# Block attention: neighbours laid beside each row from SBUF, rotation on VectorE, the sum over keys in halves

## The chip, the cores and the metric

The kernel runs on one core of a Trainium2 chip. A core has five engines that run their own instruction streams: TensorE (PE, with its weight loads as PEld), VectorE (DVE), ScalarE (ACT), GpSimd (POOL) and SyncE (SP). SP computes nothing here: it issues nearly all DMAs (SPq in the profile), in program order; an issue that waits for a semaphore holds back all those behind it. SBUF is the on-chip memory of 128 partitions, PSUM takes the matmuls' results, DRAM is outside. The metric is device time in microseconds (us) for the whole program; smaller is better.

## The reference, cut to what matters

The program is one layer with three parts: cross attention, block attention and a gated FFN, each added to x. The change lies in the block attention. There are 16 sequences of 64 rows with H = 256, so 1024 rows; 16 heads of 16 dimensions; 8 blocks a sequence, so a block has 8 rows, and each row attends to at most the 8 rows of its own block.

```python
def _L0_attn_ref(x, ...):
    bt = S // NB                                      # 64 / 8 = 8
    h = rmsnorm(x, attn_norm_w)
    qkv = bitlinear(h, qkv_w).reshape(B, S, 3, NH, HD)
    ...
    q = apply_rope(q, cos, sin)
    k = apply_rope(k, cos, sin)
    qb, kb, vb = (blk(q), blk(k), blk(v))             # blocks of bt rows
    scores = jnp.einsum('bnhqd,bnhkd->bnhqk', qb, kb) * scale
    scores = jnp.where(causal, jnp.finfo(scores.dtype).min, scores)
    attn = jax.nn.softmax(scores, axis=-1)
    ctx = jnp.einsum('bnhqk,bnhkd->bnhqd', attn, vb)
    ...
    x1 = x + bitlinear(ctx, o_w)
    hn = rmsnorm(x1, ffn_norm_w)
    gate, val = jnp.split(hn @ ffn_up_w.T, 2, axis=-1)
    return x1 + bitlinear(jax.nn.silu(gate) * val, ffn_down_w)

x = x + _L0_xattn_ref(_layernorm(x), ctx_2048, ...)   # self attention, and 1601 context keys a sequence
x = x + _L0_attn_ref(_layernorm(x), ...)
x = x + _L0_ffn_ref(x, ...)
```

`apply_rope` rotates pairs of dimensions by the row's position: x1 cos - x2 sin and x2 cos + x1 sin. `bitlinear` quantizes its input per row to 8-bit integers (`act_quant` in the kernel) and its weights to -1, 0, 1.

## The kernel before, in words

The 1024 rows are 8 tiles of 128 rows, one row on each partition. Each tile goes through the cross attention part (self attention, then 13 chunks of 128 context keys for each of four units of a tile), the block attention with its small FFN (`last_parts`, L1005), and the gated FFN. The cross attention fills TensorE: for each chunk it projects keys (`ps_k` L624), stores them to DRAM and reads them back transposed (`kd<-kh` L655, `kT<-kd` L665, both issued by SP), forms scores (`s` L696), takes running maxima on VectorE (L715), subtracts the maximum (`mx`, loaded from DRAM in L750; L754), exponentiates on ScalarE (L758) and accumulates (`acc` L772) against context rows loaded by SP (`ctxN` L617; `ctxT` L608 is the transposed copy that the projection reads). A tile's block attention is laid over the cross attention of the tile after it. Only the last tile (7) has none to lie over: there `fill()` calls put matmul chunks of the last FFN between its steps.

The order is made in two layers. All work is emitted by generators on a heap: a generator says by `yield w` how many steps later it goes on, and a list of offsets by the index of the yield (`PACE["last"]`, and `PACE["last_tile"]` for tile 7) shifts each of them. A tile framework then places the instructions on each engine's stream and adds the semaphore waits. Taking one yield out thus moves everything behind it in the same generator by a step, and each later yield takes the offset of its new index.

The block attention of a tile of rows, in order:

- L1023 and L1028: q and k (`qk`, 512 wide) and `v3` (256 wide) come from PSUM to SBUF on ScalarE.
- L1035: GpSimd multiplies `qk` by cos into `r1`; L1041: VectorE multiplies the swapped halves by sin into `r2`, two instructions of 128x256; L1046: VectorE adds them, so that `r1` holds the rotated q (first 256) and k (last 256).
- L1051: two DMAs write k (from `r1`) and v to a DRAM tile `kv`.
- L1060 (`near`): for k and for v, two tiles of 128x1024 each (one for each half of the heads) in which every row holds the 8 rows of its block side by side. A tile takes 8 DMAs: DMA k fills the partitions t = k of all 16 blocks. Each reads 16 lines of 4 KB (a block's 8 rows of 512 B lie in a row in DRAM). So 32 DMAs for each tile of rows, 64 KB each, all from SP; in tile 7 every second one of k's is issued by ScalarE instead.
- L1066 and L1067 (`product`): VectorE multiplies q by the neighbours' k and sums over the 16 dimensions into `sc` (128x128: head, key), twice; softmax L1082 to L1093; then the same function multiplies `sc` by the neighbours' v and sums over the 8 keys into `cx`, twice. The second sum reads its tile in the order head, dimension, key, so with a stride.
- L1096 to L1110: `cx` is quantized (`am`, `asc`, `aq_u`, `aq_q` L980 to L989), transposed on TensorE (`tr_aq` L997) and multiplied by the output weights (`po_o` L1110); then the FFN (`hn`, `ps_g`, `ps_u` L1129, `po_d` L1141) and in the end `out` (L1223).

The tiles `near` and `prod` share the ten buffers of the pool `wp` with the pieces of weights that SP loads.

Of the kernel before, what the change touches and what calls it, by code (L numbers as in the profile page):

```python
# [14 lines left out]
F32 = mybir.dt.float32  # L15
# [4 lines left out]
ALU = mybir.AluOpType  # L20
AX = mybir.AxisListType
PSUM = bass.MemoryType.PSUM

P = 128
B, S, H = 16, 64, 256
# [48 lines left out]
def body(tc, ctx, a):  # L74
    nc = tc.nc
    V, A, PE, GP = nc.vector, nc.scalar, nc.tensor, nc.gpsimd
# [9 lines left out]
    dram = ctx.enter_context(tc.tile_pool(name="dram", bufs=2, space=bass.MemoryType.DRAM))  # L86
# [753 lines left out]
    def fill(where):  # L840
        n = FILL.get(where, 0)
        for fn in late[:n]:
            fn()
        del late[:n]
# [97 lines left out]
    def b1(name, dt=F32):  # L942
        return one.tile([P, 256 if dt == F32 else 512], dt, tag="b1", name=name, bufs=4)

    def b2(name):
        return one.tile([P, 512], F32, tag="b2", name=name, bufs=3)
# [58 lines left out]
    def last_parts(i, start):  # L1005
        need(8, "x", i)
        last = i == NT - 1
# [4 lines left out]
        h = b1("h")  # L1012
# [14 lines left out]
        v3 = b1("v3")  # L1027
# [4 lines left out]
        if last:  # L1032
            fill("rope")
        r1, r2 = b2("r1"), b2("r2")
        GP.tensor_tensor(  # L1035
            r1.rearrange("p (h d) -> p h d", h=32), qk.rearrange("p (h d) -> p h d", h=32),
            rope[:, 0:16].unsqueeze(1).to_broadcast([P, 32, 16]), ALU.mult,
        )
# [7 lines left out]
        V.tensor_tensor(r1, r1, r2, ALU.add)  # L1046
        yield 1

        kv = dram.tile([2, 2, P, P], F32, tag="kv3", name="kv3")
        for e, t in ((0, r1[:, H : 2 * H]), (1, v3)):  # L1050
            nc.sync.dma_start(out=kv[e].rearrange("a p c -> p a c"), in_=t.rearrange("p (a c) -> p a c", a=2))  # L1051
        yield 1

        def near(e, a):
            t = wp.tile([P, 1024], F32, tag="w", name="near")
            src = kv[e, a].rearrange("(n j) c -> n (j c)", j=8)
            for k in range(8):

                q = nc.scalar if last and e == 0 and k % 2 else nc.sync
                q.dma_start(out=t.rearrange("(n t) x -> n t x", t=8)[:, k, :], in_=src)  # L1060
            return t

        def product(out, x, y, order):

            t = wp.tile([P, 1024], F32, tag="w", name="prod")
            V.tensor_tensor(t.rearrange("p (h j d) -> p h j d", h=8, j=8), x, y, ALU.mult)  # L1066
            V.reduce_sum(out, t.rearrange("p (h j d) -> p " + order, h=8, j=8), axis=AX.X)  # L1067

        near_k = [near(0, a) for a in range(2)]
        yield 2  # L1070
        sc = one.tile([P, 16, 8], F32, tag="sc3", name="sc3")
        for a in range(2):
            if last:
                fill("sc%d" % a)
            product(
                sc[:, 8 * a : 8 * a + 8, :],
                r1[:, a * P : (a + 1) * P].rearrange("p (h d) -> p h d", h=8).unsqueeze(2).to_broadcast([P, 8, 8, 16]),
                near_k[a].rearrange("p (j h d) -> p h j d", j=8, h=8), "h j d",
            )
            yield 1  # L1080
        near_v = [near(1, a) for a in range(2)]
        V.tensor_tensor(sc, sc, cmask.unsqueeze(1).to_broadcast([P, 16, 8]), ALU.add)  # L1082
        mx = small.tile([P, 16], F32, tag="mx3", name="mx3", bufs=2)
        V.reduce_max(mx, sc, axis=AX.X)
# [10 lines left out]
        cx = one.tile([P, H], F32, tag="cx3", name="cx3")  # L1095
        for a in range(2):  # L1096
            if last:
                fill("av%d" % a)
            product(
                cx[:, a * P : (a + 1) * P].rearrange("p (h d) -> p h d", h=8),  # L1100
                sc[:, 8 * a : 8 * a + 8, :].unsqueeze(3).to_broadcast([P, 8, 8, 16]),
                near_v[a].rearrange("p (j h d) -> p h j d", j=8, h=8), "h d j",
            )
            yield 1
        to = ternary_piece(1536, 512).rearrange("p (k o) -> p k o", k=2)
# [176 lines left out]
    for i in range(NT):  # L1282
        base = 52 * i
        for hh in range(2):
            for bb in range(2):
                unit(i, hh, bb, base + 26 * hh + 13 * bb)
            spawn(base + 26 * hh + 13 + 34 - 2 + (2, 1)[hh], 6.5, paced("pair", pair_out(i, hh, 4 if i < NT - 1 or hh == 0 else None)))
        ln0, sa0, qx0 = SCHEDULE[i] if i in SCHEDULE else (
            base - 22, [base + o for o in (-15, 0, 8, 21)], [base + o for o in (-16, -7, 15, 18)]
        )  # L1290
        spawn(ln0, 1.0, paced("ln" if i else "ln_first", ln_tile(i)))
        for p in range(4):
            spawn(sa0[p] - 2, 5.0, paced("sa", self_attention(i, p)))
            spawn(qx0[p] - 2, 3.0, paced("qx", queries(i, p)))
        l0 = base + {NT - 3: 95, NT - 2: 88, NT - 1: 82}.get(i, 90)
        spawn(l0, 4.5, paced("last" if i < NT - 1 else "last_tile", last_parts(i, l0)))
    spawn(-8, 1, bias_rows())
    spawn(60, 5.7, ternary())
    order = [(kind, p) for p in range(4) for kind in ("wq", "wkv", "wqx", "wproj")]
# [76 lines left out]
```

## Time and profile before

| quantity | value |
|---|---|
| median of 3 runs | 2389.42 us (2388.86 to 2392.49) |
| the profiled execution | 2387.51 us |
| its span on the core | 2385.7 us |
| instructions | 40447 |
| mean granted TensorE clock | 0.99 |
| share of the 16 DMA engines, main queue | 74.7% (682904 packets, 481.91 MB) |

The span runs from the first to the last instruction of the profiled execution; the time of the execution is 1.8 us longer. TensorE, VectorE, ScalarE, GpSimd and SyncE overlap, so shares of busy time do not add up to a time: what counts is where TensorE is idle and what ends that. The durations of the block attention's own operations, summed over all 8 tiles (the columns are line, engine, operation, tiles and shapes, count, then busy time in us and the mean of one in ns, then the idle time before them):

```profile
L1067 DVE TENSOR_REDUCE cx<-prod 128x128 f32<-128x1024 f32 x16 | 29.7, 1886 | 0.1
L1066 DVE TENSOR_TENSOR prod<-r,near 128x1024 f32<-128x1024 f32 x16 | 19.4, 1218 | 4.9 <-DMA near<-kv 4.9
L1067 DVE TENSOR_REDUCE sc<-prod 128x64 f32<-128x1024 f32 x16 | 19.3, 1211 | 0.0
L1066 DVE TENSOR_TENSOR prod<-sc,near 128x1024 f32<-128x1024 f32 x16 | 19.0, 1218 | 0.9 <-DMA out<-ot 0.8
...
L1041 DVE TENSOR_TENSOR r<-qk,shp 128x256 f32<-128x256 f32 x16 | 13.1, 826 | 6.3 <-ACT qk L1023 6.3
...
L1046 DVE TENSOR_TENSOR r<-r,r 128x512 f32<-128x512 f32 x8 | 5.5, 693 | 0.3
```
```profile
L1035 POOL TENSOR_TENSOR r<-qk,shp 128x512 f32<-128x512 f32 x8 | 10.5, 1311 | 6.8 <-ACT qk L1023 6.7
```

### The profile page before, as it was taken

To read this page: it belongs to the slowest core of one execution; us is meant where nothing else is said; L and a number is where in the kernel's file an instruction comes from. 1 tells how busy PE (TensorE), PEld (TensorE's weight loads), DVE (VectorE), ACT (ScalarE), POOL (GpSimd) and SP (SyncE) were. 2 spreads that over 40 slices of the span, in tenths; PEclk is the share of its full clock that TensorE was granted. 3 is DMA by queue.
4 is the path that set the end of the run, shared out by engine and by line. 5 is a ranking of instruction groups with operands and counts; after the bars stand their busy time and mean duration, and the time that the engine had idled before them with its cause. 6 is when DMAs were issued, how large, how long until landed. Compare 5 with 4: busy or idle time off the path is not lost.

```text
span 2385.7 us, 40447 instructions
## 1 busy us (share of the span) xinstructions
PE 2315.7 (97%) x12469; PEld 1761.8 (74%) x12477; DVE 1849.4 (78%) x4786; ACT 1663.3 (70%) x3712; POOL 755.7 (32%) x968
## 2 busy tenths in 40 slices
PE   7999999999999999999999999999999999999995
PEld 4577777777787777777777777777777777677774
DVE  7677768878878788687887779877887877876766
ACT  4677767776777777767776777777687676777620
POOL 3333223332332333332432423333333433332200
PEclk9999999999999999999999999999999999999997
DMA  8989868777977688776887769776797766965323
GB/s 263 267 236 263 235 175 240 207 186 183 269 206 196 175 229 241 197 207 181 237 224 195 203 174 260 208 196 186 185 267 199 203 174 183 262 169 141 116 85 111
DMA packets 683662, 485.18 MB, mean 203 GB/s; under 512 B 464476, under 2 KB 592952, under 8 KB 683448
## 3 DMA queue, kind: packets, MB, share of 16 engines
q1 hardware_dynamic: 682904, 481.91, 74.7%
q8 instruction: 100, 1.64, 0.3%
q14 instruction: 114, 0.93, 0.1%
q10 hardware_dynamic: 544, 0.69, 0.1%
HBM read 271.03 MB, written 113.11 MB: 161 GB/s over the span
## 4 chain that ended last, share of the span: by engine, by line
PE 79%; DVE 8%; DMA 4%; ACT 3%; issue 3%; POOL 1%; SPq 1%; ACTq 0%; DVEq 0%; POOLq 0%
PE acc L772 25%; PE ps_k L624 24%; PE s L696 14%; PE po_p L332 2%; PE po_x L863 2%; PE ps_q L379 2%; DMA kd<-kh 2%; ACT P L706 1%; PE tr_pc L799 1%; PE tr_q L399 1%; PE ps_kv L379 1%; PE sc L490 1%; DVE P L754 1%; PE pgu L1197 1%; DMA kT<-kd 1%
## 5 line engine op out<-in xcount | busy, mean ns | idle before, releaser
L772 PEld LDWEIGHTS acc<-ctxN,P 128*128 128x128 f32 (+1 forms) x4160 | 713.0, 190 | 212.5 <-issue 132.2
L772 PE MATMUL acc<-ctxN,P 128*128 128x257 f32 (+5 forms) x4160 | 799.2, 338 | 5.1 <-DMA ctxN<-in_ctx_n 2.9
L624 PE MATMUL ps_k<-wkx,ctxT 128*128 128x512 f32 x1600 | 761.1, 598 | 13.9 <-DVE wkx L1269 9.3
L567 POOL TENSOR_SCALAR vx<-ss 128x4 f32<-128x4 f32 x402 | 168.1, 418 | 1196.8 <-DVE ss L564 785.5
L706 ACT ACTIVATE P<-s,rsx 128x128 f32<-128x128 f32 x1536 | 439.6, 373 | 148.2 <-PE s L696 136.0
L568 POOL TENSOR_TENSOR rsx<-vx,nhalf 128x4 f32<-128x4 f32 x402 | 444.1, 1105 | 32.4
L624 PEld LDWEIGHTS ps_k<-wkx,ctxT 128*128 128x128 f32 x1600 | 277.8, 192 | 211.2 <-issue 190.3
L696 PE MATMUL s<-qx,kT 128*128 128x128 f32 x3072 | 411.6, 277 | 4.7 <-ACT qn L389 2.8
L696 PEld LDWEIGHTS s<-qx,kT 128*128 128x128 f32 x3072 | 377.4, 192 | 22.9 <-issue 5.3
L715 DVE TENSOR_TENSOR M<-P,M 128x512 f32<-128x512 f32 (+1 forms) x384 | 263.0, 685 | 163.1 <-ACT P L706 142.0
L651 ACT COPY kh<-ps_k 128x1024 uint16<-128x1024 uint16 x360 | 366.2, 1017 | 7.1 <-DMA kd<-kh 7.0
L758 ACT ACTIVATE P<-P 128x512 f32<-128x512 f32 (+1 forms) x416 | 266.4, 641 | 146.4 <-DVE P L754 144.8
L559 ACT ACTIVATE sq<-ps_k 128x512 f32<-128x512 f32 x402 | 242.6, 603 | 165.6 <-PE ps_k L624 141.5
L564 DVE TENSOR_REDUCE ss<-sq 128x4 f32<-128x512 f32 x402 | 272.1, 677 | 23.4 <-ACT sq L559 23.0
L754 DVE TENSOR_TENSOR P<-P,mx 128x512 f32<-128x512 f32 (+1 forms) x416 | 283.2, 681 | 0.0
L226 POOL TENSOR_TENSOR rs<-ve,nhalf 128x4 f32<-128x4 f32 (+2 forms) x112 | 116.0, 1038 | 254.0 <-DVE ve L223 239.8
L232 DVE TENSOR_SCALAR qn<-qn,mv,rs 128x128 f32<-128x128 f32 x256 | 77.2, 339 | 47.5 <-POOL rs L226 46.9
L219 DVE BATCH_NORM_STATS2 st<-qn 128x6 f32<-128x128 f32 x256 | 64.5, 271 | 21.4 <-ACT qn L389 21.3
L310 DVE TENSOR_TENSOR wproj<-wproj,w_hi 128x1024 fp32r<-128x1024 f32 x60 | 73.0, 1217 | 9.7 <-ACT w_hi L309 9.7
L309 ACT CAST w_hi<-wproj 128x1024 fp32r<-128x1024 f32 x60 | 63.3, 1056 | 24.2 <-DMA wproj<-wproj 20.4
L332 PE MATMUL po_p<-wproj,cat 128*128 128x256 f32 x272 | 67.0, 293 | 0.0
L332 PE MATMUL po_p<-w_hi,cat 128*128 128x256 f32 x240 | 65.7, 308 | 0.8 <-ACT qk L1023 0.8
(239 smaller groups left out, 2751.8 us busy)
## 6 DMA issues: line engine op xcount, KB each, us to landing
kd<-kh SPq DMA_DIRECT2D x375, 256.0 KB
ctxT<-in_ctx SPq DMA_DIRECT2D x192, 256.0 KB
ctxN<-in_ctx_n SPq DMA_DIRECT2D x384, 128.0 KB
wproj<-wproj SPq DMA_DIRECT2D x68, 512.0 KB
wq<-wq SPq DMA_DIRECT2D x32, 512.0 KB
wkv<-wkv SPq DMA_DIRECT2D x32, 512.0 KB
wqx<-wqx SPq DMA_DIRECT2D x32, 512.0 KB
near<-kv SPq DMA_DIRECT2D x248, 64.0 KB
```

Of the source, the lines that this page charges most:

```text
L332: PE.matmul(po[:, 0:H], lhsT=cat[:, h, :], rhs=w[:, h * H : (h + 1) * H], start=h + e == 0, stop=h == 3 and e == len(ws) - 1,)
L559: A.activation(sq[:n], ps[:n], AF.Square)
L564: ordered("dve", V.reduce_sum(ss[:n], sq[:n].rearrange("p (g d) -> p g d", g=4), axis=AX.X))
L568: ordered("pool", GP.tensor_tensor(rs[:n], ve[:n], nhalf[:n, 0:4], ALU.pow))
L624: PE.matmul(ps[:n, :], lhsT=st["cxT"][c // 2][:, k, o : o + n], rhs=wkx[:, k, 512 * hh : 512 * (hh + 1)], start=k == 0, stop=k == 1,)
L651: A.copy(t, src.bitcast(U16).rearrange("p (c e) -> p e c", e=2))
L696: PE.matmul(ps[:n, g * P : (g + 1) * P], lhsT=kT[:, g, 0:n], rhs=qxs[i, hh][:, bb, 2 * g : 2 * g + 2, :].rearrange("p h s -> p (h s)"), st ...
L706: A.activation(pc[:, g * P : (g + 1) * P], ps[:, g * P : (g + 1) * P], AF.Copy, scale=rs[:, g : g + 1])
L715: ordered("dve", V.tensor_tensor(st["M"][:n], pc[:n], st["M"][:n], ALU.max))
L754: ordered("dve", V.tensor_tensor(pc[:n], pc[:n], st["mx"][:n].rearrange("p g q -> p (g q)"), ALU.add))
L758: A.activation(pc[:n], pc[:n], AF.Exp)
L772: m = PE.matmul(ps, lhsT=pc[:n, g * P : (g + 1) * P], rhs=cx[:n, o : o + w], start=g < 3 and c == 0, stop=c == NC - 1, skip_group_check=g ...
```

## The change

Three things are changed in `last_parts`.

1. The product with cos moves from GpSimd (`GP`) to VectorE (`V`).
2. The DRAM tile `kv`, its two writes and the `yield 1` behind them are gone. `near` reads its neighbours from SBUF, from `r1` or `v3`: a DMA takes all 128 partitions of one half of the heads (128 floats, 512 B each) and writes them as 16 lines of 8 pieces. A DMA still moves 64 KB, in 128 pieces of 512 B where it was 16 of 4 KB. The number of DMAs, their engines and the alternation in tile 7 stay. The entries of the lists `PACE["last"]` and `PACE["last_tile"]` are not edited, so the yields behind the removed one take the entries one place earlier.
3. The sum over the 8 keys (`cx`) is made of three additions on the product's own tile: 64 + 64 elements for each of 8 heads (512 in all), then 32 + 32 (256), then 16 + 16 (128) into `cx`. The sum over dimensions (`sc`) stays a reduction.

```diff
--- before.py
+++ after.py
@@ -1032,7 +1032,7 @@
         if last:
             fill("rope")
         r1, r2 = b2("r1"), b2("r2")
-        GP.tensor_tensor(
+        V.tensor_tensor(
             r1.rearrange("p (h d) -> p h d", h=32), qk.rearrange("p (h d) -> p h d", h=32),
             rope[:, 0:16].unsqueeze(1).to_broadcast([P, 32, 16]), ALU.mult,
         )
@@ -1046,39 +1046,37 @@
         V.tensor_tensor(r1, r1, r2, ALU.add)
         yield 1
 
-        kv = dram.tile([2, 2, P, P], F32, tag="kv3", name="kv3")
-        for e, t in ((0, r1[:, H : 2 * H]), (1, v3)):
-            nc.sync.dma_start(out=kv[e].rearrange("a p c -> p a c"), in_=t.rearrange("p (a c) -> p a c", a=2))
-        yield 1
-
-        def near(e, a):
+        def near(src, a, both):
             t = wp.tile([P, 1024], F32, tag="w", name="near")
-            src = kv[e, a].rearrange("(n j) c -> n (j c)", j=8)
             for k in range(8):
 
-                q = nc.scalar if last and e == 0 and k % 2 else nc.sync
-                q.dma_start(out=t.rearrange("(n t) x -> n t x", t=8)[:, k, :], in_=src)
+                q = nc.scalar if both and k % 2 else nc.sync
+                q.dma_start(
+                    out=t.rearrange("(n t) (j c) -> n t j c", t=8, j=8)[:, k], in_=src[:, a * P : (a + 1) * P]
+                )
             return t
 
-        def product(out, x, y, order):
+        def product(x, y):
 
             t = wp.tile([P, 1024], F32, tag="w", name="prod")
             V.tensor_tensor(t.rearrange("p (h j d) -> p h j d", h=8, j=8), x, y, ALU.mult)
-            V.reduce_sum(out, t.rearrange("p (h j d) -> p " + order, h=8, j=8), axis=AX.X)
-
-        near_k = [near(0, a) for a in range(2)]
+            return t
+
+        near_k = [near(r1[:, H : 2 * H], a, last) for a in range(2)]
         yield 2
         sc = one.tile([P, 16, 8], F32, tag="sc3", name="sc3")
         for a in range(2):
             if last:
                 fill("sc%d" % a)
-            product(
-                sc[:, 8 * a : 8 * a + 8, :],
+            t = product(
                 r1[:, a * P : (a + 1) * P].rearrange("p (h d) -> p h d", h=8).unsqueeze(2).to_broadcast([P, 8, 8, 16]),
-                near_k[a].rearrange("p (j h d) -> p h j d", j=8, h=8), "h j d",
+                near_k[a].rearrange("p (j h d) -> p h j d", j=8, h=8),
+            )
+            V.reduce_sum(
+                sc[:, 8 * a : 8 * a + 8, :], t.rearrange("p (h j d) -> p h j d", h=8, j=8), axis=AX.X
             )
             yield 1
-        near_v = [near(1, a) for a in range(2)]
+        near_v = [near(v3, a, False) for a in range(2)]
         V.tensor_tensor(sc, sc, cmask.unsqueeze(1).to_broadcast([P, 16, 8]), ALU.add)
         mx = small.tile([P, 16], F32, tag="mx3", name="mx3", bufs=2)
         V.reduce_max(mx, sc, axis=AX.X)
@@ -1096,10 +1094,14 @@
         for a in range(2):
             if last:
                 fill("av%d" % a)
-            product(
-                cx[:, a * P : (a + 1) * P].rearrange("p (h d) -> p h d", h=8),
+            t = product(
                 sc[:, 8 * a : 8 * a + 8, :].unsqueeze(3).to_broadcast([P, 8, 8, 16]),
-                near_v[a].rearrange("p (j h d) -> p h j d", j=8, h=8), "h d j",
+                near_v[a].rearrange("p (j h d) -> p h j d", j=8, h=8),
+            ).rearrange("p (h x) -> p h x", h=8)
+            for n in (64, 32):
+                V.tensor_tensor(t[:, :, 0:n], t[:, :, 0:n], t[:, :, n : 2 * n], ALU.add)
+            V.tensor_tensor(
+                cx[:, a * P : (a + 1) * P].rearrange("p (h d) -> p h d", h=8), t[:, :, 0:16], t[:, :, 16:32], ALU.add
             )
             yield 1
         to = ternary_piece(1536, 512).rearrange("p (k o) -> p k o", k=2)
```

## The prediction

> **What bounds the kernel now.** I read the busy line first, then a table of stretches, one for each row tile of 128 rows (columns: PE, PEld, DVE, ACT and POOL busy, granted clock, DMA share, GB/s).
>
> ```profile
> PE 2315.7 (97%) x12469; PEld 1761.8 (74%) x12477; DVE 1849.4 (78%) x4786; ACT 1663.3 (70%) x3712; POOL 755.7 (32%) x968
> ```
> ```profile
> 740.00:1025.00 285.00, 282.47 (x1555) 217.33 (x1555) 228.29 (x591) 209.10 (x464) 94.12 (x119) 1.00 0.78 210
> ...
> 2163.00:2280.00 117.00, 112.28 (x637) 90.73 (x637) 79.95 (x152) 74.53 (x174) 26.00 (x34) 0.97 0.44 129
> 2280.00:2386.00 106.00, 79.66 (x395) 63.20 (x394) 63.88 (x160) 15.42 (x32) 3.60 (x5) 0.88 0.28 89
> ```
>
> PE is idle for 70 us of 2385.7: 26 in the last 106, 4.7 in the stretch before, 17 at the start. A middle stretch of 285 loses only 1.5 to 4. The change deletes no matmul, so it can be paid only in idle PE time that block attention causes. Two views find that time. Windows of 10 us:
>
> ```profile
> 870.00:880.00 10.00, 8.62 (x52) 6.68 (x51) 9.36 (x20) 6.87 (x15) 1.37 (x2) 1.00 1.12 264
> ```
>
> The same window in six tiles (from 585, 870, 1155, 1440, 1715, 2020) has PE busy 8.01, 8.62, 9.51, 8.85, 8.68, 8.07: 8.3 us lost in all. SP's timeline and the chain of waits say why:
>
> ```profile
> 853.46 10.54 SPq L1060 DMA_DIRECT2D near<-kv  x16
> ...
> 864.72 1.45 SPq L665 DMA_TRANSPOSE kT<-kd  x1
> ```
> ```profile
> 867.83 6.45 DMA kT<-kd
> ```
>
> Sixteen loads of v's neighbours hold SP for 10.5 us; the transposes of context keys (kT) queued behind them start late, and the scores on PE wait for one (867.83 to 874.28). DVE meanwhile runs the four operations of the v product (L1066, L1067) without a break, 6 us, which holds back the softmax work that PE needs. The second place is tile 6, window 2265 to 2275 (PE 6.28 of 10): PE's waits give 4.0 us at tr_aq L997 for DVE's aq_q L989, the quantizer behind cx. The third is the tail, below.
>
> **The change part by part. The tail (tile 7), where little covers it.** The chain and the timeline of before:
>
> ```profile
> 2328.49 0.36 SPq L1051 DMA_DIRECT2D kv<-r  x1
> ...
> 2330.37 15.30 SPq L1060 DMA_DIRECT2D near<-kv  x24
> ```
> ```profile
> 2345.08 2.24 DMA near<-kv
> ...
> 2348.06 1.24 DVE prod L1066
> 2349.32 1.87 DVE cx L1067
> 2351.21 0.43 DVE am L980
> ```
>
> 24 issues on SP (8 of k, 16 of v) take 15.30, or 0.637 each; ScalarE's queue issues the other 8 of k. The last lands 2.24 us after its issue, then DVE multiplies, sums, quantizes.
> (a) Rotation. Before: POOL's product 1.27 (L1035) beside two halves that took 1.66 instead of 2 x 0.42, then the sum 0.69. After, all on DVE: 0.60 (128x512, start to start) + 0.34 + 0.34 = 1.28, plus one late FFN operation (0.34) that the new order puts between: 1.62. r1 is ready as before: 0.
> (b) The hop through DRAM. kv<-r starts at 2328.49, near at 2330.33: 1.84 vanish, gain 1.8. The loads' own issue has no row for SBUF to SBUF in 16x8x128. Bounds: 0.348 and 0.351 (kd<-kh and out<-ot, which read SBUF) and 0.844 (the longest near on ScalarE's queue), plus the 0.045 gap; I take the near row itself, 0.587, as it has the same size and writes the same tile. At 0.40 an issue the tail gains another 24 x 0.24 = 5.7 at most, but DVE's own chain (k products, softmax to 2344.1, v products) then ends it, so about 1.3; at 0.89 it loses 24 x 0.25 = 6.1.
> (c) The landing. 128 packets of 512 B for 16 of 4 KB. Bounds: kv<-r, 256 packets of 512 B, has the next load issued 1.83 after its own issue began; near took 2.24 to 2.50. I take 2.24: 0, with -0.4 to +0.3.
> (d) The sum over keys. A strided reduce is 1.886; three additions are 0.685 (L715, 512 elements) + 0.42 (256, a half of L1041 that ran alone) + 0.28 (128, L1082) = 1.39: 0.5 less. Only the second sum is on the path: gain 0.45. If strides slow additions as they slow the reduce (1.886 against 1.211 for the contiguous sc<-prod), 1.39 x 1.56 = 2.17: loss 0.3.
> Tail: 1.8 + 0.45 = 2.2 gain, between -6 and +4.
>
> The Trainium skill ("VectorE: DVE Perf Modes", Rules for kernel authors) advises to minimize the number of chained DVE operations, which speaks against three for one, though the same table calls tensor_reduce the slowest operation. By the first rule (d) would be a loss; the rows here give the gain above. The skill ("DMA: Bandwidth & Descriptors", Rules for kernel authors) says that the tile's shape can make 128 small descriptors of 16 large ones, eight times as many at an eighth of the size, and that which is faster was not measured. No run of before shows it for these bytes.
>
> **Middle tiles (0 to 6).** DVE per tile: +0.69 (r1's product), -0.9 (one of L1041's pair took 1.31 instead of 0.42 beside POOL's product), -2 x 0.5 (sums): 1.2 less of some 228. DVE is not full (80%), so this counts only where PE waits for it. POOL loses 1.3 of 94: nothing waits there. SP loses two kv writes, 0.36 + 0.37. What counts is where the 32 loads stand, which are issued a step sooner since a yield is gone. As built, the changed kernel issues k's neighbours two, one, then a burst of 13 in tile 1 (before 1, 2, 2, 1, 1, 1 and 8). v's 16 stay one burst, but the newest kT stands ahead of it and context loads follow. By 0.635 each the k burst is 8.3 us; a kT that had stood ahead of 12 of these loads stands behind them, 7.6 later. Behind the v burst the next kT comes 4.5 late (one whose keys are ready only then) instead of 11.3. The rows above price such delays: 864.72 less 853.46, 11.3 us, cost PE 1.38, so about 10 us are absorbed by kT's lead. Both new delays lie below 10: the burst's stall goes. DVE's v product no longer comes as a 6 us block (the two halves stand some 12 instructions apart). I do not take all 8.3: half may be DVE work that PE waits for elsewhere, or the k burst may take a little back. Gain 4, between 0 and 8.3. The extra packets: 28,672 more, 4,096 fewer. Mean time of a packet is 74.7% x 16 x 2385.7 / 682,904 = 42 ns, so 24,576 x 42 ns / 16 = 65 us of engine share at most, 2.7 points on some 75%, less what the 4 KB packets took; it lengthens landings only where the share is already full (1.12 in that window). Price if it bites: one us a tile.
> Tile 6: v's product now precedes part of the late softmax work, so the 4.0 us wait for aq_q shrinks; but 12 k loads stand ahead of the mx load (6 to 8 us later) and 16 between context loads. Gain 1.5, between +3.7 and -3.
>
> Sum: 4 + 1.5 + 2.2 = 7.7. The profiled execution took 2387.51 (span 2385.7 and 1.8 around it), which is 1.9 below the median of the runs. 2387.5 - 7.7 = 2379.8; on the median's level 2381.7. I say **2382**.
>
> **The rivals.**
> 1. Only the tail gains (chance 0.27). The middle is 99% PE and what is freed in one window is lost in the next. For it: windows beside the six lose 0.7 to 0.9 at ps_g, which the change does not touch. Against: SP's burst is the releaser by name. 2389.4 - 2.2, less 0 to 2: 2385 to 2387.
> 2. Slower (0.17): SP's issue. If an SBUF to SBUF load of 128 pieces costs SP 0.9 instead of 0.635, the k burst is 13 x 0.9 = 11.7 and passes the 10 us of lead: 1.7 a tile for seven tiles = 12, less the old stall's 8.3, plus 24 x 0.26 - 2.2 = 4.1 in the tail: +8, 2397. It decides from 10 / 13 = 0.77 us an issue. For it: single near issues of before reach 1.61. Against: kd and out, with 128 partitions of SBUF as source, issue in 0.35.
> 3. All stalls go (0.13): 8.3 + 3.7 + 3.5 in the tail (issue near 0.40) = 15.5: 2374. For it: the 0.35 rows. Against: half of the six windows' loss need not be SP's.
>
> **How the numbers follow.** The forecast has 0.43, its own range 2377 to 2386. Under 0.2% (4.8 us) a measurement of this kernel cannot tell from no change: faster is below 2384.6, slower above 2394.2. Faster: most of 0.43, all of rival 3: 0.53. Same: rival 1 and a rest of the forecast: 0.31. Slower: 0.16. The range takes in rival 3 and the beginning of rival 2: 2372 to 2395.
>
> **What would show it.** Right: first near of the tail within 0.3 us of r1's sum, near issues at 0.5 to 0.65; three additions of about 1.4 in sum; L1041's halves both at 0.42; PE above 9.3 in the windows behind the v burst; end of cx some 2.2 us earlier. Wrong: an issue above 0.77 us, PE waiting for kT in the k burst or for mx or ctxN in tile 6, landings above 4 us.

## The result, and the profile after

The changed kernel takes 2405.37 us (median of 6 runs, 2400.39 to 2407.09) beside 2389.14 for the kernel before (6 runs, 2381.82 to 2392.49): a ratio of 1.0074, 95% interval 1.0061 to 1.0088. It is slower by 16 us by the medians (18 by the ratio) where 7 were to be gained. Its profiled execution took 2405.49 with a span of 2403.6, 17.9 more than the span of before.

The busy line of the page:

```profile
PE 2323.4 (97%) x12477; PEld 1764.5 (73%) x12477; DVE 1834.2 (76%) x4826; ACT 1660.8 (69%) x3712; POOL 757.5 (32%) x960
```

DVE has 15 us less to do, more than the forecast's 9.6, and PE does no more work: its 7.7 more busy us are the same matmuls (8 more records of them), which take longer around the waits; in three of the windows further down the granted clock is 0.85, 0.83 and 0.73, where all six windows of before had 1.00. So idle time of DVE is worth nothing here, as the forecast had it, and the loss has to be looked for in PE's waits.

VectorE's groups (line, engine, operation, tiles, shapes, count, busy us, mean ns, idle time before):

```profile
L1102 DVE TENSOR_TENSOR prod<-prod 128x512 f32<-128x512 f32 x16 | 11.0, 685 | 0.1
L1102 DVE TENSOR_TENSOR prod<-prod 128x256 f32<-128x256 f32 x16 | 6.7, 416 | 0.1
L1103 DVE TENSOR_TENSOR cx<-prod 128x128 f32<-128x128 f32 x16 | 4.5, 284 | 0.1
```

Each sum over keys is now 0.685 + 0.416 + 0.284 = 1.385 us instead of 1.886. The pair of L1041 takes 0.415 each, not 0.826.

Where the time went is seen by taking the start of the same instruction in both traces: the n-th weight load of the key projection `ps_k`, of which each trace has 1608 (1600 of L624, 8 of L582; us; worked out from the two traces):

```
n                      384    608    800    992   1184   1408   1600
before                 515    837   1108   1382   1650   1965   2235
changed, later by     +1.0   +5.7   +8.7  +12.5  +17.0  +19.5  +22.4
```

Between two columns, about a tile of rows apart, 2.5 to 4.7 us are lost, 22.4 by the time that tile 6 is nearly through, and 4.5 of them are won back behind that (22.4 less 17.9). Of the 22.4, 13 are idle time of PE and 9 are its busy time, the same matmuls taking longer (worked out from the two traces). PE's waits tell what is new (engine and line that waits, engine and line waited for: us in all, times, longest):

```profile
PE tr_aq L997 <- DVE aq_q L989: 20.6, 7, 13.0
...
PE ps_k L624 <- ACT kh L651: 6.9, 7, 2.3
PE ps_kv L379 <- ACT w_hi L309: 6.0, 5, 2.0
```

The same two of before:

```profile
PE tr_aq L997 <- DVE aq_q L989: 18.6, 3, 13.4
...
PE ps_k L624 <- ACT kh L651: 2.8, 1, 2.8
```

Before, ps_kv had no such wait, and the three at tr_aq lay in tile 6 and in the tail. So there are two new places in each of the tiles 0 to 4. SP's timeline of tile 1 shows the first, before and after:

```profile
842.89 0.43 SPq L301 DMA_DIRECT2D wkv<-wkv  x1
...
853.07 0.34 SPq L655 DMA_DIRECT2D kd<-kh  x1
853.46 10.54 SPq L1060 DMA_DIRECT2D near<-kv  x16
```
```profile
846.52 0.58 SPq L301 DMA_DIRECT2D wq<-wq  x1
847.20 10.64 SPq L1054 DMA_DIRECT2D near<-v  x16
...
859.06 0.41 SPq L655 DMA_DIRECT2D kd<-kh  x1
859.56 0.38 SPq L301 DMA_DIRECT2D wkv<-wkv  x1
```

The burst of v's loads is as long as before, but other things stand behind it: a store of keys (kd) and the weights wkv of the next self attention, which before were issued ahead of it. ScalarE's timeline shows what that does:

```profile
862.20 1.01 ACT L651 COPY kh<-ps_k 128x1024 uint16<-128x1024 uint16 x1 [2.47 <-DMA kd<-kh]
864.14 1.04 ACT L309 CAST w_hi<-wkv 128x1024 fp32r<-128x1024 f32 x1 [0.93 <-DMA wkv<-wkv]
```

The brackets hold the idle time before an instruction and its releaser. The copy of keys `kh` has no free buffer until the late store has landed, and behind it, in ScalarE's order, stands the split of wkv, which waits for its load. PE waits for both:

```profile
863.26 1.12 PE L624 MATMUL ps_k<-wkx,ctxT 128*128 128x512 f32 x2 [0.45 <-ACT kh L651]
865.24 0.39 PE L379 MATMUL ps_kv<-w_hi,xq 128*128 128x256 f32 x1 [0.85 <-ACT w_hi L309]
```

The windows of 10 us at this place in six tiles (the window and its length, then the columns of the forecast's table):

```profile
570.00:580.00 10.00, 7.33 (x33) 5.56 (x34) 4.67 (x14) 5.16 (x10) 0.00 (x0) 0.85 1.11 272
860.00:870.00 10.00, 8.15 (x42) 5.91 (x43) 6.90 (x17) 6.35 (x12) 1.74 (x2) 1.00 1.04 280
1148.00:1158.00 10.00, 6.73 (x38) 4.89 (x37) 5.19 (x13) 5.25 (x11) 0.00 (x0) 1.00 0.99 267
1438.00:1448.00 10.00, 7.77 (x34) 5.94 (x33) 5.81 (x16) 5.74 (x12) 0.52 (x2) 0.83 1.18 267
1720.00:1730.00 10.00, 8.44 (x48) 6.20 (x47) 7.22 (x19) 6.72 (x13) 2.26 (x4) 1.00 1.04 260
2030.00:2040.00 10.00, 5.93 (x25) 4.72 (x24) 7.92 (x16) 5.95 (x12) 3.13 (x4) 0.73 0.97 268
```

PE loses 15.7 us in them where the kernel before lost 8.3 in its six. The second place lies some 60 us later: PE waits 1.2 to 1.8 us a tile at tr_aq for the quantizer of the FFN (`sg`). VectorE's timeline of tile 3:

```profile
1499.69 0.68 DVE L1136 SCALAR_TENSOR_TENSOR sg<-sg,ps_g 128x512 f32<-128x512 f32 x1
1500.28 1.22 DVE L310 TENSOR_TENSOR wproj<-wproj,w_hi 128x1024 fp32r<-128x1024 f32 x1
1501.42 0.68 DVE L1137 SCALAR_TENSOR_TENSOR sg<-sg,ps_u 128x512 f32<-128x512 f32 x1
1502.02 1.22 DVE L310 TENSOR_TENSOR wqx<-wqx,w_hi 128x1024 fp32r<-128x1024 f32 x1
1503.15 0.68 DVE L980 TENSOR_REDUCE am<-sg 128x1 f32<-128x512 f32 x1
```

Two splits of weights (L310, 1.22 each) now stand in the way, one between the FFN's two products and one between the second product and the first step of the quantizer. Before, these three followed each other directly:

```profile
1484.38 0.68 DVE L1134 SCALAR_TENSOR_TENSOR sg<-sg,ps_g 128x512 f32<-128x512 f32 x1
1485.17 0.69 DVE L1135 SCALAR_TENSOR_TENSOR sg<-sg,ps_u 128x512 f32<-128x512 f32 x1
1485.89 0.69 DVE L980 TENSOR_REDUCE am<-sg 128x1 f32<-128x512 f32 x1
```

The first place adds 7.4 us of idle PE (15.7 less 8.3), the second 6.6 (the waits at tr_aq in tiles 0 to 4). That is about the 13 above; the other 9 of the 22.4 are the longer matmuls.

The tail went as foreseen. The chain of waits of the changed kernel:

```profile
2362.77 2.09 DMA near<-v
...
2365.60 1.24 DVE prod L1062
...
2368.37 0.43 DVE am L980
```

From the start of qk's copy to the quantizer's `am` the kernel before took 2351.21 - 2325.01 = 26.2 us, the changed one 2368.37 - 2344.85 = 23.5: 2.7 less.

### The profile page after: what moved, and what is told of

Read it like the earlier page. It is cut to its first block, busy times and chain, and to the rows that moved or that the text cites. A ratio compares the mean times of both kernels' runs of the same rounds, so it can differ in the third digit from the quotient of the medians.

```text
span 2403.6 us, 40447 instructions
## 1 busy us (share of the span) xinstructions
PE 2323.4 (97%) x12477; PEld 1764.5 (73%) x12477; DVE 1834.2 (76%) x4826; ACT 1660.8 (69%) x3712; POOL 757.5 (32%) x960
## 3 DMA queue, kind: packets, MB, share of 16 engines
q1 hardware_dynamic: 706328, 479.81, 75.4%
## 4 chain that ended last, share of the span: by engine, by line
PE 74%; DVE 10%; DMA 5%; ACT 4%; issue 3%; SPq 2%; POOL 2%; ACTq 0%; DVEq 0%; POOLq 0%
PE acc L772 24%; PE ps_k L624 22%; PE s L696 13%; PE po_p L332 2%; PE ps_q L379 2%; DMA mx<-rowd 2%; PE po_x L863 2%; SPq L1054 1%; ACT P L706 1%; DMA wkv<-wkv 1%; PE tr_pc L799 1%; DVE P L754 1%; PE ps_kv L379 1%; PE sc L490 1%; PE tr_q L399 1%
## 5 line engine op out<-in xcount | busy, mean ns | idle before, releaser
L624 PE MATMUL ps_k<-wkx,ctxT 128*128 128x512 f32 x1600 | 762.6, 598 | 17.9 <-DVE wkx L1271 9.2
L568 POOL TENSOR_TENSOR rsx<-vx,nhalf 128x4 f32<-128x4 f32 x402 | 451.5, 1123 | 32.9
L624 PEld LDWEIGHTS ps_k<-wkx,ctxT 128*128 128x128 f32 x1600 | 278.0, 192 | 214.2 <-issue 188.0
L226 POOL TENSOR_TENSOR rs<-ve,nhalf 128x4 f32<-128x4 f32 (+2 forms) x112 | 121.3, 1085 | 264.9 <-DVE ve L223 245.8
L310 DVE TENSOR_TENSOR wproj<-wproj,w_hi 128x1024 fp32r<-128x1024 f32 x60 | 72.9, 1217 | 9.7 <-ACT w_hi L309 9.5
```

The costliest lines, as they stand in the source:

```text
L568: ordered("pool", GP.tensor_tensor(rs[:n], ve[:n], nhalf[:n, 0:4], ALU.pow))
L624: PE.matmul(ps[:n, :], lhsT=st["cxT"][c // 2][:, k, o : o + n], rhs=wkx[:, k, 512 * hh : 512 * (hh + 1)], start=k == 0, stop=k == 1,)
```

## The experiments

The two theories. Theory 1 (order): the three edits are sound, but with the DRAM hop a `yield 1` went out too, so every later step of the block attention stands one step earlier, its yields take other offsets of the list, and the framework's order has other things behind the burst and before the quantizer. The rival (transfer): 128 pieces of 512 B cost more than 16 of 4 KB and hold the other loads up, whatever the order.

**Only the yield taken out of the kernel before.**

```diff
             nc.sync.dma_start(out=kv[e].rearrange("a p c -> p a c"), in_=t.rearrange("p (a c) -> p a c", a=2))
-        yield 1
```

> The kernel before with nothing changed but the one yield behind the kv writes taken out: DRAM hop, GpSimd product and strided sum stay. Theory 1: slower by 14 to 22 us, 2403 to 2412, with PE waiting for w_hi at ps_kv. Rival (transfer): within 4 us of before.

2411.14 beside 2391.10, ratio 1.0085 (1.0068 to 1.0101). None of the three edits is in this kernel, and it is slower by 20 us. Its waits are those of the changed kernel: at ps_kv for w_hi 5.1 us in 5, at ps_k for kh 7.2 in 7, at tr_aq 30.0 in 7 (1.3 to 2.7 in each of the tiles 0 to 4; 19.5 in one wait of the tail, where the changed kernel has 13.0). SP's order in tile 1 is the new one too: the burst of v's loads, here from DRAM, starts at 844.48 and takes 10.51, kd follows at 856.20 and wkv at 856.71, and ScalarE's copy `kh` stands idle for 2.62 until a kd has landed. So the yield alone makes a loss of this size, at the same places. Whether the three edits on top of it give something back is not shown: the two intervals overlap.

**The edits with the yield kept.** First the loads alone, in the kernel before (the DRAM tile and its two writes go, the yield stays):

```diff
-        kv = dram.tile([2, 2, P, P], F32, tag="kv3", name="kv3")
...
         yield 1
...
-            src = kv[e, a].rearrange("(n j) c -> n (j c)", j=8)
+            src = (r1[:, H : 2 * H], v3)[e][:, a * P : (a + 1) * P]
...
-                q.dma_start(out=t.rearrange("(n t) x -> n t x", t=8)[:, k, :], in_=src)
+                q.dma_start(out=t.rearrange("(n t) (j c) -> n t j c", t=8, j=8)[:, k], in_=src)
```

> The kernel before with part 2 alone and with its yield kept: neighbours from SBUF in 128 pieces of 512 B, no DRAM tile, no kv writes; GpSimd's product and the strided sum stay. Theory 1: the loads' form costs nothing that shows and the hop of 1.8 us in the tail is gone: 2384 to 2391. Rival (transfer): 24,576 more packets, at 42 ns on 16 engines some 8 us a tile of DMA time in the bursts, delay kT and ctxN: 2396 to 2406.

2383.05 beside 2390.45, ratio 0.9967 (0.9954 to 0.9979): 7.4 us faster, 1 below the stated 2384 to 2391. The rival falls. The same 128-piece loads that the changed kernel has, in the order of before, are a gain.

Then the two VectorE edits alone, in the kernel before:

```diff
-        GP.tensor_tensor(
+        V.tensor_tensor(
             r1.rearrange("p (h d) -> p h d", h=32), qk.rearrange("p (h d) -> p h d", h=32),
...
-            product(
...
+            t = wp.tile([P, 1024], F32, tag="w", name="prod")
+            V.tensor_tensor(
...
+            t = t.rearrange("p (h x) -> p h x", h=8)
+            for n in (64, 32):
+                V.tensor_tensor(t[:, :, 0:n], t[:, :, 0:n], t[:, :, n : 2 * n], ALU.add)
+            V.tensor_tensor(
+                cx[:, a * P : (a + 1) * P].rearrange("p (h d) -> p h d", h=8), t[:, :, 0:16], t[:, :, 16:32], ALU.add
+            )
```

(the call of `product` is replaced for `cx` alone; `sc` keeps it).

> The kernel before with parts 1 and 3 alone: product with cos on VectorE and the sum over keys in three additions; DRAM tile, its two writes and the yield stay. Theory 1: the parts are sound, DVE gets about 1.2 us a tile and the tail 0.5 us: 2383 to 2391, 0 to 7 below before. Rival (the DVE parts shift work that PE waits for): 2395 or more.

2391.77 beside 2390.45, ratio 1.0009 (1.0000 to 1.0019): no gain and hardly a loss, just above the stated 2383 to 2391. The 0.5 us of the tail do not show against the rest.

Each VectorE edit beside the loads, yield kept: the changed kernel with `yield 1` back, once with the product on GpSimd, once with the strided reduction.

> Parts 2 and 3 with the yield kept: neighbours from SBUF and the sum over keys in three additions; the product with cos stays on GpSimd. The loads alone came to 2383 beside 2390.5 for before. Theory 1 with the additions a gain: 2378 to 2383 (0.45 us in the tail and up to 0.9 at each tr_aq of a middle tile). If the additions displace work that PE waits for: 2385 to 2391. The transfer rival is not what this asks.

> Parts 2 and 1 with the yield kept: neighbours from SBUF and the product with cos on VectorE; the sum over keys stays one strided reduction. If moving the product is free or better (1.66 us of the slowed pair against 0.69 + 0.76): 2380 to 2384. If it costs what the two DVE parts together seemed to cost beside before (+0.1%, 0 to 0.2): 2385 to 2391.

2385.02 (ratio 0.9964, 0.9949 to 0.9978) and 2385.18 (0.9970, 0.9957 to 0.9982), both beside 2392.42. As plain times both fall into the second branch, 2385 to 2391. But before was 2 us slower in this comparison, and by the ratios neither adds or takes anything that can be told from the loads alone (0.9967): neither the gain expected of the additions nor a cost showed. All three edits together with the yield in its old place were not run.

**Which step of the yield matters.** Three kernels with all three edits. First, v's loads one yield later and nothing else:

```diff
-        near_v = [near(v3, a, False) for a in range(2)]
...
         A.activation(sc, sc, AF.Exp, scale=0.25)
         yield 1
+        near_v = [near(v3, a, False) for a in range(2)]
```

> The changed kernel with v's neighbours loaded one yield later (behind the exponential), so that wq, wkv and two kT stand ahead of the burst; all other steps stay where the change put them. Theory 1 has two parts: wkv behind the burst (about 2 to 3 us a tile, ps_kv's gap and its stretched matmuls) and the shifted FFN quantizer (1.2 to 1.8 us a tile). If the first is the larger: 2387 to 2396. If it is the quantizer alone: 2402 to 2406. Rival (transfer): 2402 to 2406.

2406.31 beside 2391.10, ratio 1.0065 (1.0047 to 1.0083): no better than the changed kernel, 10 us above the first branch and at the edge of the other two. But the wait has changed its place:

```profile
PE tr_aq L997 <- DVE aq_q L989: 33.4, 14, 12.4
```

The waits at ps_kv for w_hi are gone, as expected of wkv ahead of the burst. In their place PE waits 1.0 to 2.4 us in each of the tiles 0 to 4 for cx's quantizer, and the FFN's quantizer is still late. In tile 1 the last load of the burst is issued by 871.47, and VectorE's two v products stand at 871.65 and 877.09 in its order, among the work on maxima. VectorE is not seen to wait for these loads in the middle tiles; so by the timelines the order made with the later loads holds the quantizer, not a late landing. So the branches, which priced one of two waits as gone, were too simple: a burst moved out of the way of one load moves its own readers too.

Second, a yield behind the sums into cx, so that quantizers and FFN stand as before:

```diff
         to = ternary_piece(1536, 512).rearrange("p (k o) -> p k o", k=2)
         yield 1
+        yield 1
```

> The changed kernel with a yield added behind the sums into cx, so that the quantizers, the output projection and the FFN stand in their steps of before, while the loads, the scores and the softmax stay one step early and the v burst stays ahead of wkv. Theory 1: the waits at tr_aq for the FFN's quantizer go, those for w_hi stay: 2394 to 2401. If the quantizer is the whole loss: 2384 to 2390. Rival (transfer): 2402 to 2406.

2398.40 (12 runs, 2393.28 to 2407.93) beside 2391.10, ratio 1.0038 (1.0024 to 1.0052): by the medians about half of the loss comes back. Its waits in the middle tiles are those of the first place:

```profile
PE ps_kv L379 <- ACT w_hi L309: 7.4, 5, 2.2
PE ps_k L624 <- ACT kh L651: 5.8, 6, 2.2
```

No wait at tr_aq is left there. The two places are thus separate: this run has the first without the second, the run before it the second without the first. How the loss divides between them is less sure. The profiled execution took 2405.66, the third longest of the twelve and as long as the changed kernel's, so its waits do not explain the median of 2398; and no run takes away the first place alone.

Third, the yield behind the loads of k's neighbours, so that only these stand early:

```diff
         near_k = [near(r1[:, H : 2 * H], a, last) for a in range(2)]
         yield 2
+        yield 1
```

> The changed kernel with one yield added behind the loads of k's neighbours: these loads stay one step early (burst of 13), everything behind them, v's loads, softmax, quantizers and FFN, stands in its step of before. The two experiments before moved the loss from one wait to the other (v's loads later: waits for w_hi at ps_kv gone, those for the quantizer at tr_aq up to 33 us; FFN realigned: the reverse). Theory 1 (the lost yield is the whole loss, by both waits together): both waits go, 2380 to 2390. Rival (transfer: the 128-piece loads themselves cost, or the early burst of k): 2396 or more.

2391.08 beside 2390.45, ratio 0.9996 (0.9983 to 1.0008): the whole loss is gone (1 us above the stated 2380 to 2390), though the 7 us that the loads give with the yield in its old place are not there. The burst of v's loads now stands behind qb, kd and a kT, and the waits for w_hi at ps_kv are gone. But PE now waits 2.9 us in each of the tiles 0 to 4 for cx's quantizer (tr_aq 28.9 in 8), so "both waits go" did not come true as it was meant. In the measure of the table of starts this kernel is 6.4 us late at n = 1600 and makes up 5.7 of that in tile 6 and the tail (worked out from the two traces): the old time is reached by another way.

**Splitting the burst.** On the kernel of 2383, the second tile of v's neighbours one yield later:

```diff
-        near_v = [near(1, a) for a in range(2)]
+        near_v = [near(1, 0)]
...
         A.activation(sc, sc, AF.Exp, scale=0.25)
         yield 1
+        near_v.append(near(1, 1))
```

> Neighbours from SBUF alone (the kernel of 2383) with the second tile of v's neighbours loaded one yield later, so that qb and one kT stand between two bursts of 8. Theory 1 (a burst costs by what waits behind it): kT comes 5 us sooner, the remaining waits at acc and s behind the burst (0.4 to 1.0 a tile) shrink, but the second product is 2 us later: 2379 to 2384. If the later loads hold back cx's quantizer as they did when all 16 were moved (2.1 to 2.9 a tile at tr_aq): 2388 to 2395.

2426.70 beside 2392.42, ratio 1.0137 (1.0119 to 1.0156): far worse than either branch. PE waits 7.6 us in each of the tiles 0 to 4 for cx's quantizer:

```profile
PE tr_aq L997 <- DVE aq_q L989: 49.5, 7, 10.2
```

In VectorE's order both v products (883.99 and 887.02 in tile 1) stand behind a running maximum, and that one waits 5.8 us for ScalarE:

```profile
882.18 0.69 DVE L715 TENSOR_TENSOR M<-P,M 128x512 f32<-128x512 f32 x1 [5.83 <-ACT P L706]
```

What made ScalarE late there was not followed further.

**Moving wkv instead of the burst.** On the kernel of 2398 (FFN realigned), the load of wkv one yield earlier, directly ahead of the burst; and the same move in the kernel before as a control:

```diff
+        w_kv = weights("wkv", p) if i else [raw_piece("wkv", p)]
         yield 1
-        w_kv = weights("wkv", p) if i else [raw_piece("wkv", p)]
         w_q = halved(w_q)
```

> The kernel with the FFN realigned (2398 beside 2391 for before; waits of PE for w_hi 7.4 us in 5, none at tr_aq in the middle) and one more edit: the self attention loads wkv together with wq, one yield earlier, so that it stands directly ahead of the burst of v's loads, which itself stays. Theory 1 (what is left of the loss is wkv behind the burst): the waits for w_hi go, 2386 to 2393. Rival (the burst delays kd, kT and ctxN just as much, and PE waits there): 2396 or more, with the wait moved to acc, ps_k or s.

> The control: the kernel before with the same move of wkv's load, one yield earlier, and nothing else. There wkv stands ahead of the burst anyway, so its earlier load should be worth nothing: 2388 to 2394. If it gains more than 4 us by itself, the run with wkv ahead of the burst has to be read less that gain.

The first took 2432.72 beside 2390.40, ratio 1.0174 (1.0153 to 1.0195), the control 2408.60, ratio 1.0070 (1.0055 to 1.0085). By number and place the first lies in the rival's branch, but the timeline below gives another reason than the burst; the control missed its 2388 to 2394. In the first the waits for w_hi are gone and a larger one is there:

```profile
PE ps_k L624 <- ACT kh L651: 39.1, 7, 6.9
```

In each of the tiles 0 to 4 PE waits 6.9 us at one place. ScalarE's timeline of tile 1 says why the copy of keys is late:

```profile
877.13 0.63 ACT L758 ACTIVATE P<-P 128x512 f32<-128x512 f32 x1 [4.23 <-DVE P L754]
877.67 1.91 ACT L651 COPY kh<-ps_k 128x1024 uint16<-128x1024 uint16 x2
```

It stands behind an exponential that waits for VectorE, where the splits of wq and wkv and the first v product now follow each other. The control tells that the move is not neutral either, at 18 us by itself, so the first run cannot settle what wkv's place is worth. That wkv and kd behind the burst are what costs at the first place rests on the timelines and on the run with v's loads later, in which those waits went but the time did not fall.

## Why the prediction was wrong, step by step

- **Bound.** Right: PE sets the time, DVE's 15 us less are worth nothing by themselves (the run with the two VectorE edits alone: ratio 1.0009), and the burst of v's loads on SP is the place to look at.
- **(a) rotation, tail.** Right: 0.69 + 0.75 + 0.68 in place of 1.66 + 0.69; from the start of qk's copy to the end of r1's sum 3.1 us, before 3.45: a gain of 0.35 for a forecast 0.
- **(b) the hop and the price of an issue.** Right: the first near is issued at 2347.97, r1's sum ends at 2347.94. 24 issues of SP take 15.36 us from first to last, 0.64 each (forecast 0.635); the median issue is 0.597, before 0.587. The bounds of 0.35 and 0.84 were both far off.
- **(c) landing.** 2.09 us, before 2.24: no cost.
- **(d) the sum over keys.** 1.385 for a forecast 1.39. With (b) the tail gained 2.7 up to the quantizer, 1.9 up to the end (from qk's copy 60.7 before, 58.75 now); forecast 2.2.
- **Tile 6.** From the last column of the table of starts to the tail's qk the lag shrinks from 22.4 to 19.8: a gain of 2.6, forecast 1.5. The wait for aq_q in tile 6, 4.0 before, is gone. A part may be the clock, for which the sum had no term: the window of before with that wait had 0.66 granted, the changed kernel has 1.00 throughout this stretch.
- **Middle tiles: here the forecast failed**, in the sentences "Both new delays lie below 10: the burst's stall goes" and "Gain 4, between 0 and 8.3". Instead of a gain of 4, PE was 22.4 us late by the end of these tiles. The sentences price the burst by the delay of one kind of instruction behind it, kT, and kT indeed is no longer waited for there, save once for 1.8 us in tile 5. What else had come to stand behind the burst was not priced: the text itself says that "context loads follow", and did not go on to kd, whose store frees the buffer that the next copy of keys needs, and wkv, behind which ScalarE and PE stand in order. That cost 15.7 us of PE in the six windows instead of 8.3, a mean of 7.39 busy where the text wanted more than 9.3. And the FFN was taken to stay where it was: the removed yield moved its steps too, and the 1.2 to 1.8 us a tile at tr_aq are a term that the sum did not have, nor are the 9 us by which PE's matmuls grew longer. The run with the yield alone taken out, +20 us with the same waits, shows that both places come from the yield. That it is kd and wkv behind the burst, and the two splits before the quantizer, is read from the timelines.
- **The packets.** The main queue has 23,424 packets more (706328 for 682904), all queues 24,320 (forecast 24,576). It went from 74.7% of 2385.7 us to 75.4% of 2403.6, some 30 us of engine share more where the text allowed 65. No price of it shows: the three kernels with these packets and the yield in its old place were the fastest.
- **The rivals.** The slower one came true in sign, but not by its mechanism (issue price 0.9). A rival for "a removed yield re-orders what lies behind the burst" was missing, and the lower bound of the middle tiles, 0, had no reason that excluded a loss.

## What to carry to other kernels

Where a program's order follows from counted steps, an edit that takes out a step is two changes, and the second can be the larger: here the loads from SBUF with the step kept were worth -7 us, and the lost step without any edit +20. Run the edit with the step kept in place, and the lost step without the edit, before judging either. When a burst of issues moves on a queue, list everything that then stands behind it, with the reader of each, and price all of them: stores that free buffers and weights for another part count as much as the transfer that waited last time.

## What was not expected of the hardware

A DMA of 64 KB from SBUF to SBUF in 128 pieces of 512 B cost SyncE the same to issue as one of 16 lines of 4 KB from DRAM (0.597 and 0.587 us, medians of 248), and the last one of the tail landed in 2.09 us where the other took 2.24. Eight times as many pieces of an eighth of the size did not show in the time. The source differs too, SBUF for DRAM, so these runs do not price the pieces alone.
